# Two graph attention layers over 2708 nodes: weight rows on ScalarE's DMA queue, and layer 0 started with block 1

## The chip, the cores and the metric

The kernel runs on one core of one Trainium2 chip. Five engines with instruction streams of their own share the core's memory: TensorE (PE, matrix products), VectorE (DVE), ScalarE (ACT), GpSimd (POOL) and SyncE (SP). Transfers are issued by SP, ACT or POOL and carried by 16 DMA engines. The metric is device time in microseconds (us); smaller is better.

## The reference

Both layers work on 2708 nodes of 1024 float32 features, and on one symmetric 0/1 adjacency matrix in which about 0.6% of the entries are set, the diagonal always.

```python
# layer 0
f = x @ Wf + bf;  g = x @ Wg + bg
e = relu(f @ g.T)
attention = softmax(where(adj > 0, e, NEG), axis=1)
x = layernorm(x + attention @ (x @ W + bW))
# layer 1
h = x @ W1;  f1 = h @ a1;  f2 = h @ a2
e = leaky_relu(f1 + f2.T, 0.2)
attention = softmax(where(adj > 0, e, NEG), axis=1)
x = layernorm(x + relu(attention @ h))
```

## The kernel before

**Algebra.** Only the scores of neighbours are needed. Since f·g of a pair is a row of `x @ (Wf Wg^T)` (plus a row of constants) times a row of x, plus a number of the row alone, the kernel makes `M = Wf Wg^T` once, and per block of nodes one product F = xM. A score is then the dot product of a row of F with the gathered x of a neighbour.

**The stage before layer 0** (lines 194 to 500) does two things side by side. `lists(b)`, for each of 22 blocks of 128 rows of adj, loads 1354 KB (`sp.dma_start`, L405, into one of three buffers), marks the entries on ACT (`act.activation`, L407), multiplies by a ramp on POOL (L409), and picks the neighbours out on DVE (L412 to L418). `weights()` is a generator with one step per block: `turned` takes 128 rows of a weight (tile `rows`, three buffers), turns them on PE and copies the result to SBUF on ACT; `m_product(k, h)` makes a 128x512 piece of M out of 16 matmuls. `load_weights` issues the row loads two ahead, on SP (L276). So SP's queue holds, in program order, adj loads and weight rows mixed. `row_parts` on POOL splits a row (of the bias bW, and of a product with biases) into three bf16 rows; its float32 inputs and rests use the three buffers of tile `rest`. The two halves of bW are loaded at the start of `weights()` (L348 to L352).

**Order.** `InOrder` (L61) keeps the instructions of the five engines named `pe`, `dve`, `act`, `pool` and `sp` in program order, each engine for itself. The `nc.vector` and `nc.gpsimd` instructions of `lists` and `row_parts` are placed among them by the planner of the language.

**Layer 0** (lines 690 to 904). The sorted nodes are cut into block 0 of 20 nodes (32 rows, 3 gathered tiles) and 21 blocks of 128 rows in four groups of 32 rows. A tile is 128 gathered rows of x (`gather`, POOL), and 20 of them fit into `ring`; the order of gathers is that of `units`, and a slot is taken again once `sums` has read it. Per block: `load_x` fetches its rows (`xb`, one buffer), `q_dot` and `q_spread` make the number of the row alone (DVE, PE, DVE), `x_turn` turns xb on PE and copies it on ACT, `f_product` makes F into PSUM, `replicate(b, k)` copies the 32 rows of group k to all four quarters of a tile `Fr` (four ACT copies), `dots` forms the scores on DVE, one instruction per tile, `soft` makes the softmax weights (with an exponential on ACT), `sums` weighs the gathered tiles on PE, ACT scales them into `y`, `turn` turns y, `product` with Wt = W gives the rows of `x @ W`, and `close` adds x and normalises. Iteration k of the loop (L832) treats block b = k: its sums, the product with W of block b - 1 (`back`), x_turn and F of block b + 2 (`ahead`), and dots and softmax of block b + 1. Block 0 needs only one Fr; `f_small` spreads the inner dimension of its F over the four quarters of PE, copies these parts (`parts`) and adds them with a matmul by `rep`.

Transposes and small results go to `ps_t`, two PSUM buffers, and F and products to `ps_m`, two as well.

**Layer 1** (lines 907 to 992) is of the same make, with the products after the sums, and its rows come from a table T1 that layer 0 writes.

Of the kernel before, what the change touches and what calls it, by code (L numbers as in the profile page):

```python
# [8 lines left out]
F32 = mybir.dt.float32  # L9
# [97 lines left out]
def listed_path(ctx, tc, x, adj, Wf, bf, Wg, bg, W, bW, W1, a1, a2, out):  # L107
# [16 lines left out]
    Q = 4  # L124
# [69 lines left out]
    with tc.tile_pool(name="pre", bufs=1) as pre:  # L194
# [54 lines left out]
        with tc.tile_pool(name="adjp", bufs=3) as adjp, tc.tile_pool(name="cands", bufs=2) as cands, \  # L249
                tc.tile_pool(name="wt", bufs=1) as wt, tc.tile_pool(name="stage", bufs=3) as stage:  # L250

            def row_parts(rest, dst):

                for i in range(3):
                    t = pre.tile([1, 512], BF16, name="part", bufs=2)
                    nc.gpsimd.tensor_copy(t, rest)
                    nc.gpsimd.dma_start(dst[i:i + 1], t)
                    if i < 2:
                        nxt = pre.tile([1, 512], F32, name="rest", bufs=3)
                        nc.gpsimd.tensor_tensor(nxt, rest, t, op=ALU.subtract)  # L260
                        rest = nxt
# [10 lines left out]
            def load_weights(upto):  # L272
                while len(loaded) < min(upto, len(order)):
                    w, k = order[len(loaded)]
                    t = stage.tile([P, D], F32, name="rows")
                    sp.dma_start(t, w[k * P:(k + 1) * P, :])  # L276
                    loaded.append(t)

            at = iter(range(len(order)))
# [12 lines left out]
            def weights():  # L292
# [52 lines left out]
                four = pre.tile([32, P], F32, name="four")  # L345
                for i, v in enumerate((bg, bf, a1, a2)):
                    act.dma_start(four[8 * i:8 * i + 8], v.rearrange("(k p) -> k p" if i < 2 else "(k p) o -> k (p o)", p=P))
                for h in range(H):  # L348
                    half = slice(h * 512, (h + 1) * 512)
                    brow = pre.tile([1, 512], F32, name="rest", bufs=3)  # L350
                    act.dma_start(brow, bW[half].rearrange("(o d) -> o d", o=1))
                    row_parts(brow, b3[:, half])  # L352
                cols = pre.tile([P, 4, KC], F32, name="cols")
                bgc, bfc, ac = cols[:, 0, :], cols[:, 1, :], cols[:, 2:4, :]
                WgT = {0: half_tile()}
# [7 lines left out]
                for k in range(KC):  # L363
                    flush()
                    turned(WfT[:, :, k * P:(k + 1) * P])
                    if k >= 4:
                        turned(WgT[1][:, :, (k - 4) * P:(k - 3) * P])
                    m_product(k, 0)
                    yield
                flush()  # L370
                c_product(0)
# [155 lines left out]
    def product(n, xT, w, row=None):  # L527
# [9 lines left out]
                          start=(row is None and k == 0), stop=(k == KC - 1))  # L537
        return pm

    flat = lambda pm: pm.rearrange("p h d -> p (h d)")  # L540

    def scatter(table, idx, src):
# [28 lines left out]
    class Unit:  # L571
        pass

    def cut(most, turns):


        units, at = [], 0
        for b in range(NB):
            u = Unit()
            u.b, u.gs, u.at = b, groups[b], at  # L580
            u.G, u.T, u.n = len(u.gs), max(TILES[g] for g in u.gs), nrows[b]
            u.tiles = [(k, g, t) for k, g in enumerate(u.gs) for t in range(TILES[g])]
            u.col = {(k, t): m for m, (k, g, t) in enumerate(u.tiles)}
            u.tiles.sort(key=lambda m: (m[0] // turns, m[2]))
            u.sc = scores[b % 2][:, :u.G, :u.T]
            assert len(u.tiles) <= min(most, MOST)
            at += len(u.tiles)
            units.append(u)
        return units
# [101 lines left out]
    with ExitStack() as s0s:  # L691
# [2 lines left out]
        tp, frp = new_pool("tp", 2), new_pool("frp", Q)  # L694
        stp, xp, yp, jp = (new_pool(n, 1) for n in ("stp0", "xp", "yp", "jp0"))
        zs = new_pool("zp", 1).tile([P, TW], F32, name="z")
        units = cut(R0, 2)
        lay = Layer(units, [ring], D, x, stp)
        xb, q, qd, F, Fr, xTs, yTs, Wp, y, Z = ({} for _ in range(10))

# [30 lines left out]
        def f_small():  # L731


            xT = xTs.pop(0)
            pm = ps_m.tile([P, H, 512], F32, name="pm")
            for h in range(H):
                c = slice(h * 512, (h + 1) * 512)
                pe.matmul(pm[:32, h, :], ones3[0:3, :32], c3[:, c], start=True, stop=False)
                for k in range(KC // Q):
                    for p in range(Q):  # L740
                        i = p * KC // Q + k
                        pe.matmul(pm[32 * p:32 * p + 32, h, :], xT[:, i, :32], M[:, i, c],
                                  start=(k == 0 and p > 0), stop=(k + 1 == KC // Q))
            parts = frp.tile([P, D], F32, name="Fr")
            act.copy(parts, flat(pm))
            yield
            pm = ps_m.tile([P, H, 512], F32, name="pm")
            for h in range(H):
                pe.matmul(pm[:, h, :], rep, parts[:, h * 512:(h + 1) * 512], start=True, stop=True)
            Fr[0, 0] = frp.tile([P, D], F32, name="Fr")  # L750
            act.copy(Fr[0, 0], flat(pm))

        def replicate(b, k):
# [36 lines left out]
                pool.memset(z[:, D + 1:], 0.0)  # L790
            scatter(T1[:, :], ids[:m, b:b + 1], z[:m])

        load_x(0)
        load_x(1)
        load_lists(0)
        load_lists(1)

        def first_gathers(g0, g1):

            dve.tensor_scalar(SL0[:, g0:g1], SL[:, g0:g1, :], float(N - 1), None, op0=ALU.min)  # L800
            lay.gathers()

        q_dot(0)
        q_dot(1)
        lay.most = len(units[0].tiles)
        first_gathers(0, 1)
        lay.most += len(units[1].tiles)
        first_gathers(1, 5)
        x_turn(0)
        spread0, spread1 = q_spread(0), q_spread(1)  # L810
        next(spread0)
        small_f = f_small()
        next(small_f)
        x_turn(1)
        for _ in small_f:
            pass
        next(spread1)
        f_product(1)
        pool.memset(zs[:, D:], 0.0)
        load_x(2)  # L820
        load_lists(2)
        load_lists(3)
        for steps in (spread0, spread1):
            for _ in steps:
                pass
        for k in range(2):
            replicate(1, k)
        act.dma_start(Wt, W.rearrange("(k p) d -> p k d", p=P))
        dots(units[0], 0, len(units[0].tiles))
        soft(units[0])  # L830
        closing, loaded = iter(()), None
        for k, u in enumerate(units):  # L832
            nxt = units[k + 1] if k + 1 < len(units) else None
            b = u.b
            back = b - 1 if b > 0 else None
            ahead = b + 2 if b + 2 < NB else None
            po = ps_s.tile([P, H, 512], F32, name="po")
            y[b] = yp.tile([P, D], F32, name="y")
            if back is not None:
                for _ in yTs[back][1]:  # L840
                    pass
            reps = list(range(len(groups[b + 1]))) if nxt is not None else []

            first = k == 0
            for r in reps[2:] if first else reps[:1]:
                replicate(b + 1, r)
            next(closing, None)
            if loaded is not None:
                q_dot(loaded)
                loaded = None  # L850
            next(closing, None)
            for r in [] if first else reps[1:3]:
                replicate(b + 1, r)
            lay.sums(u, po, {12: [lambda s=closing: [None for _ in s]]})
            closing = iter(())
            act.activation(y[b][:u.n], flat(po)[:u.n], AF.Copy, scale=u.ri[:u.n])
            if ahead is not None:
                x_turn(ahead)
            if b + 3 < NB:
                load_x(b + 3)  # L860
                loaded = b + 3
            if back is not None:
                load_residual(back)
                Wp[back] = product(nrows[back], yTs.pop(back)[0], Wt, 32)
            spreading = iter(())
            if ahead is not None and not first:
                spreading = q_spread(ahead)
                next(spreading)
            for r in [] if first else reps[3:]:
                replicate(b + 1, r)  # L870
            if ahead is not None:
                f_product(ahead)
            if ahead == NB - 1:
                sp.dma_start(M, W1.rearrange("(k p) d -> p k d", p=P))
            yT = tp.tile([P, KC, P], F32, name="xT")
            steps = turn(y[b], nrows[b], yT)
            next(steps)
            yTs[b] = yT, steps
            if b + 4 < NB:
                load_lists(b + 4)  # L880
            if nxt is not None:
                dots(nxt, 0, len(nxt.tiles))
            for _ in spreading:
                pass
            if nxt is not None:
                soft(nxt)
            if first:
                q_dot(ahead)
                for _ in q_spread(ahead):
                    pass  # L890
                lay.most = len(lay.order)
                first_gathers(5, NSL0)
            if back is not None:
                closing = close(back)
                next(closing)
# [11 lines left out]
    with ExitStack() as s1s:  # L907
# [4 lines left out]
        x1 = [rb, u1b]  # L912
        z1 = [u2b, zp.tile([P, D], F32, name="z1")]
        more = new_pool("ring1", 1).tile([P, R1 - R0, TW], F32, name="more")
        units = cut(R1, Q)
        lay = Layer(units, [ring, more], TW, T1[:, :], stp)
        prod, yTs, y = {}, {}, {}

# [454 lines left out]
```

## Time and profile before

| | |
|---|---|
| median of 5 runs | 1829.52 us (1825.91 to 1834.27) |
| the profiled execution | 1834.62 us; span in the trace 1832.8 us; mean granted PE clock 0.953 |
| busy: PE, DVE, ACT, POOL | 1638.9, 1171.9, 623.6, 1189.2 us |
| stage before layer 0, up to the first gather | 0 to 242.3 us |
| start of layer 0, up to the turn of block 4's rows | 242.3 to 372.5 us |
| layer 0 from there to its end | to about 1200 us; PE busy 39.7 of each 40 us in most of it |
| moved by the DMA engines | 501.82 MB |

A line of the timeline has the start and the duration in us, the engine (SPq and ACTq are DMA issues), the source line (L71 for everything that `InOrder` records), the operation, out<-in with shapes, and in brackets the idle time of the engine before it and what ended it. A line of the waits has who waited for whom, the total in us, how often, and the longest. A line of the windows has start:end, the length, busy us of PE, PE's weight loads, DVE, ACT and POOL, and then the granted PE clock, the DMA share and GB/s.

### The profile page before, as it was taken

To read this page: it belongs to the slowest core of one execution; us is meant where nothing else is said; L and a number is where in the kernel's file an instruction comes from. 1 tells how busy PE (TensorE), PEld (TensorE's weight loads), DVE (VectorE), ACT (ScalarE), POOL (GpSimd) and SP (SyncE) were. 2 spreads that over 40 slices of the span, in tenths; PEclk is the share of its full clock that TensorE was granted. 3 is DMA by queue.
4 is the path that set the end of the run, shared out by engine and by line. 5 is a ranking of instruction groups with operands and counts; after the bars stand their busy time and mean duration, and the time that the engine had idled before them with its cause. 6 is when DMAs were issued, how large, how long until landed. Compare 5 with 4: busy or idle time off the path is not lost. (4 is left out here: it accounts for less than half of the span.)

```text
span 1832.8 us, 22235 instructions
## 1 busy us (share of the span) xinstructions
PE 1638.9 (89%) x6965; PEld 678.3 (37%) x6965; DVE 1171.9 (64%) x3533; ACT 623.6 (34%) x757; POOL 1189.2 (65%) x1191
## 2 busy tenths in 40 slices
PE   3999568899999999999999999738999999899995
PEld 2444223233444444444444444312333333333442
DVE  2868946878888888888898887523334424424442
ACT  3544516334454544444454555100111111111110
POOL 7558754666666666666667664047777777777741
PEclk8999878899999999999999999868999999999998
DMA  5555255667777777777767787269999999999960
GB/s 214 204 189 217 105 183 196 210 209 248 272 295 284 289 268 272 288 266 280 261 258 265 269 292 308 94 242 374 351 396 398 391 369 392 382 396 386 373 238 30
DMA packets 149979, 501.82 MB, mean 274 GB/s; under 512 B 32565, under 2 KB 32597, under 8 KB 147144
## 3 DMA queue, kind: packets, MB, share of 16 engines
q0 software_dynamic: 132032, 427.36, 63.1%
q1 hardware_dynamic: 13658, 68.30, 9.8%
q10 hardware_dynamic: 4162, 4.65, 0.7%
q8 instruction: 57, 0.93, 0.2%
q14 instruction: 70, 0.57, 0.1%
HBM read 509.64 MB, written 33.75 MB: 296 GB/s over the span
## 5 line engine op out<-in xcount | busy, mean ns | idle before, releaser
L71 POOL DMA_INDIRECT ring<-in_x_dram,SL x405 | 439.8, 1086 | 247.9 <-issue 96.0
L71 DVE SCALAR_TENSOR_TENSOR j<-ring,Fr 128x1024 bf16<-128x1024 f32 x405 | 497.8, 1229 | 92.6 <-DMA ring<-in_x_dram,SL 73.8
L71 PE MATMUL po<-ring,st 128*32 128x512 f32 x2660 | 386.0, 615 | 0.2 <-issue 0.2
L71 ACT COPY Fr<-pm 32x1024 f32<-32x1024 f32 (+1 forms) x338 | 339.1, 1003 | 27.0 <-PE pm L71 22.5
L71 POOL DMA_INDIRECT ring<-T,SL x260 | 258.5, 994 | 85.9 <-issue 45.2
L71 PE MATMUL pm<-Wt,xT 128*128 128x512 f32 (+1 forms) x704 | 313.7, 598 | 0.0
L71 PE MATMUL pm<-M,yT 128*128 128x512 f32 (+1 forms) x704 | 307.9, 595 | 0.3 <-ACT yT L71 0.3
L71 PE MATMUL pm<-M,xT 128*128 128x512 f32 (+1 forms) x704 | 305.3, 610 | 0.3 <-ACT xT L71 0.3
L71 ACT ACTIVATE scores<-scores 128x24 f32<-128x24 f32 (+5 forms) x44 | 9.8, 222 | 651.7 <-DVE scores L71 651.7
L71 PEld LDWEIGHTS pm<-M,yT 128*128 128x128 f32 (+1 forms) x704 | 129.5, 186 | 178.2 <-issue 177.6
L71 PEld LDWEIGHTS po<-ring,st 128*32 128x32 f32 x2660 | 111.4, 114 | 226.2 <-issue 222.1
L71 PEld LDWEIGHTS pm<-Wt,xT 128*128 128x128 f32 (+1 forms) x704 | 127.6, 186 | 159.5 <-issue 159.3
L71 PEld LDWEIGHTS pm<-M,xT 128*128 128x128 f32 (+1 forms) x704 | 125.2, 188 | 153.4 <-issue 152.8
L71 POOL DMA_INDIRECT more<-T,SL x145 | 144.6, 997 | 44.7 <-issue 27.7
L409 POOL TENSOR_TENSOR adj<-adj,iota 128x2708 f32<-128x2708 f32 (+3 forms) x23 | 130.4, 5676 | 53.2 <-ACT adj L71 53.2
L71 DVE TENSOR_SCALAR scores<-ring,f1q 128x2 f32<-128x2 f32 (+5 forms) x98 | 21.8, 237 | 200.7 <-DMA ring<-T,SL 200.4
L412 DVE MAX8 cand<-adj 128x8 f32<-128x136 f32 (+2 forms) x440 | 97.1, 285 | 56.8 <-POOL adj L409 56.8
L71 ACT ACTIVATE y<-po,ri 128x1024 f32<-128x1024 f32 (+1 forms) x44 | 49.0, 1113 | 237.2 <-PE po L71 228.5
L71 PE MATMUL pm<-halfT,WfT 128*128 128x512 f32 x256 | 117.8, 617 | 8.9 <-ACT WfT L71 8.9
L71 POOL DMA_INDIRECT SL<-LD,idq x85 | 88.1, 1037 | 25.9 <-issue 21.0
L71 PE MATMUL po<-more,st 128*32 128x512 f32 x580 | 97.8, 627 | 0.0
L71 PE MATMUL pt<-rs,stack 128*32 128x1 f32 x340 | 10.9, 182 | 86.0 <-DVE rs L71 57.7
(190 smaller groups left out, 1397.1 us busy)
## 6 DMA issues: line engine op xcount, KB each, us to landing
adj<-in_adj_dram SPq DMA_DIRECT2D x21, 1354.0 KB
X1S<-z SPq DMA_DIRECT2D x20, 512.0 KB
ring<-in_x_dram,SL POOLq DMA_INDIRECT x405, 6.2
u1b<-X1S SPq DMA_DIRECT2D x11, 512.0 KB
rb<-X1S SPq DMA_DIRECT2D x10, 512.0 KB
ring<-T,SL POOLq DMA_INDIRECT x260, 6.8
rows<-in_L_gnn_Wg_dram SPq DMA_DIRECT2D x8, 512.0 KB
rows<-in_L_gnn_Wf_dram SPq DMA_DIRECT2D x8, 512.0 KB
```

Of the source, the lines that this page charges most:

```text
L71: made = self.tc.keep_in_program_order(op(*args, **kwargs))
L409: nc.gpsimd.tensor_tensor(k[:n, cut], k[:n, cut], iota[:n, cut], op=ALU.mult)
L412: nc.vector.max(cand[:n, s, :], k[:n, s * SEG:min((s + 1) * SEG, N)])
```

## The change

- **Weight rows.** `load_weights` issues its 24 loads on ACT; SP's queue of this stage holds the 22 adj loads alone.
- **bW.** The load and the `row_parts` of each half of bW move from the start of `weights()` into its steps k = 2 and k = 5.
- **Order of layer 0.** `cut` takes an order, here 1, 0, 2, 3, ..., and the loop takes `back`, `ahead` and `nxt` from it. Loads, lists, x_turn and F of block 1 come ahead of those of block 0. x_turn(2) and F(2) move ahead of the loop. In the first iteration (now block 1) x_turn, F, and the product with W are left out; q of block 2 and `load_x(3)` come at its end, after the lists of block 4. The gathers of block 2 are released ahead of the first softmax instead of at the end of the first iteration.
- **F of block 1** is copied as 32 copies of 32x512, columns 0 to 511 of all four groups first; in the second half, group 1 is copied by DVE and the rest by ACT.
- **`f_small`** uses a general `split_product`, run through at once by `whole`, after F(1) and its copies; its parts go to the buffer of `y` and its result to `zs`.

```diff
-                    sp.dma_start(t, w[k * P:(k + 1) * P, :])
+                    act.dma_start(t, w[k * P:(k + 1) * P, :])
...
-                for h in range(H):
-                    half = slice(h * 512, (h + 1) * 512)
-                    brow = pre.tile([1, 512], F32, name="rest", bufs=3)
-                    act.dma_start(brow, bW[half].rearrange("(o d) -> o d", o=1))
-                    row_parts(brow, b3[:, half])
...
                     m_product(k, 0)
+                    if k in (2, 5):
+                        half = slice(k // 3 * 512, k // 3 * 512 + 512)
+                        brow = pre.tile([1, 512], F32, name="rest", bufs=3)
+                        act.dma_start(brow, bW[half].rearrange("(o d) -> o d", o=1))
+                        row_parts(brow, b3[:, half])
                     yield
...
+    def split_product(xT, w, parts, row=None):
+        pm = ps_m.tile([P, H, 512], F32, name="pm")
+        for h in range(H):
+            c = slice(h * 512, (h + 1) * 512)
+            if row is not None:
+                pe.matmul(pm[:32, h, :], ones3[row:row + 3, :32], rows3[row:row + 3, c], start=True, stop=False)
+            for k in range(KC // Q):
+                for p in range(Q):
+                    i = p * KC // Q + k
+                    pe.matmul(pm[32 * p:32 * p + 32, h, :], xT[:, i, :32], w[:, i, c],
+                              start=(k == 0 and (row is None or p > 0)), stop=(k + 1 == KC // Q))
+        act.copy(parts, flat(pm))
+        yield
+        pm = ps_m.tile([P, H, 512], F32, name="pm")
+        for h in range(H):
+            pe.matmul(pm[:, h, :], rep, parts[:, h * 512:(h + 1) * 512], start=True, stop=True)
+        return pm
+
+    def whole(steps):
+        while True:
+            try:
+                next(steps)
+            except StopIteration as end:
+                return end.value
...
-        units = cut(R0, 2)
+        seq = [1, 0, *range(2, NB)]
+        units = cut(R0, 2, seq)
...
+            pm = whole(split_product(xTs.pop(0), M, yp.tile([P, D], F32, name="y"), 0))
+            Fr[0, 0] = zs[:, :D]
             act.copy(Fr[0, 0], flat(pm))
...
+        load_x(1)
+        load_x(0)
+        load_lists(1)
+        load_lists(0)
+        q_dot(1)
         q_dot(0)
-        q_dot(1)
         lay.most = len(units[0].tiles)
+        first_gathers(1, 5)
+        x_turn(1)
+        spread0, spread1 = q_spread(0), q_spread(1)
+        next(spread1)
+        load_x(2)
+        load_lists(2)
+        lay.most += len(units[1].tiles)
         first_gathers(0, 1)
...
         x_turn(0)
...
         f_product(1)
         pool.memset(zs[:, D:], 0.0)
-        load_x(2)
-        load_lists(2)
         load_lists(3)
-        for steps in (spread0, spread1):
+        next(spread0)
+        for steps in (spread1, spread0):
             for _ in steps:
                 pass
-        for k in range(2):
-            replicate(1, k)
+
+        for k in range(Q):
+            Fr[1, k] = frp.tile([P, D], F32, name="Fr")
+        for h in range(H):
+            c = slice(h * 512, (h + 1) * 512)
+            for k in range(Q):
+                take = dve.tensor_copy if h > 0 and k == 1 else act.copy
+                for p in range(Q):
+                    take(Fr[1, k][32 * p:32 * p + 32, c], F[1][32 * k:32 * k + 32, h, :])
+        f_small()
+        x_turn(2)
+        f_product(2)
         act.dma_start(Wt, W.rearrange("(k p) d -> p k d", p=P))
         dots(units[0], 0, len(units[0].tiles))
+        lay.most = len(lay.order)
+        first_gathers(5, NSL0)
         soft(units[0])
...
-            if ahead is not None:
+            if ahead is not None and not first:
                 x_turn(ahead)
...
-            if ahead is not None:
+            if ahead is not None and not first:
                 f_product(ahead)
...
                 q_dot(ahead)
                 for _ in q_spread(ahead):
                     pass
-                lay.most = len(lay.order)
-                first_gathers(5, NSL0)
+                loaded = seq[k + 3]
+                load_x(loaded)
```

## The prediction

> **What bounds the kernel now.** The windows say that the bulk of layer 0 is PE-bound (39.7 busy us of 40), so what counts is when that stretch is reached. I therefore read the timeline of the two stretches ahead of it, and the waits of SP's queue in the first.
>
> ```profile
> 420.00:460.00 40.00, 39.71 (x159) 15.75 (x159) 34.51 (x79) 16.50 (x19) 24.79 (x25) 1.00 0.66 228
> ```
>
> ```profile
> SPq L71 <- PE pt L71: 96.7, 16, 16.2
> ```
>
> ```profile
> 21.37 1.07 ACT L71 COPY halfT<-pt 128x512 f32<-128x512 f32 x2 [10.91 <-POOL rest L260]
> ...
> 26.18 0.42 SPq L71 DMA_DIRECT2D adj<-in_adj_dram  x1
> ...
> 34.14 2.46 ACT L71 ACTIVATE adj<-adj 128x2708 f32<-128x2708 int32 x1 [6.05 <-DMA adj<-in_adj_dram]
> ...
> 37.22 8.86 PE L71 MATMUL pm<-halfT,WfT 128*128 128x512 f32 x16 [8.07 <-ACT WfT L71]
> ...
> 71.87 0.33 SPq L71 DMA_DIRECT2D rows<-in_L_gnn_Wg_dram  x1
> 72.30 0.37 SPq L71 DMA_DIRECT2D adj<-in_adj_dram  x1
> ...
> 79.02 2.46 ACT L71 ACTIVATE adj<-adj 128x2708 f32<-128x2708 int32 x1 [5.12 <-DMA adj<-in_adj_dram]
> ...
> 83.69 1.15 PE L71 MATMUL pt<-ident,rows 128*128 128x128 f32 x8 [2.67 <-ACT WfT L71]
> ...
> 106.88 1.97 PE L71 MATMUL pt<-ident,rows 128*128 128x128 f32 x8 [3.43 <-ACT WfT L71]
> ...
> 206.93 2.46 ACT L71 ACTIVATE adj<-adj 128x2708 f32<-128x2708 int32 x1 [2.03 <-POOL rest L260]
> ```
>
> ACT stands 10.9 us behind the second half of bW; PE's transposes stand with it, SP's next weight row waits for them, and adj of block 1, next in SP's queue, goes out at 26.2. M starts at 37.2. At 72.3 and again later adj follows a weight row by 0.4 us; ACT and then PE wait. From 108.6 to 211.5 PE hardly stops. The lists end at 231.
>
> ```profile
> 272.11 4.04 ACT L71 COPY Fr<-pm 32x1024 f32<-32x1024 f32 x4 [13.87 <-PE pm L71]
> ...
> 281.40 7.83 PE L71 MATMUL po<-ring,st 128*32 128x512 f32 x12 [0.21 <-issue]
> ...
> 305.91 1.00 POOL L71 DMA_INDIRECT xb<-in_x_dram,ids  x1 [18.63 <-PE pt L71]
> ...
> 310.25 1.23 DVE L71 SCALAR_TENSOR_TENSOR j<-xb,rb 128x1024 bf16<-128x1024 f32 x1 [3.35 <-DMA xb<-in_x_dram,ids]
> ...
> 348.23 1.11 PE L71 MATMUL pt<-ident,y 128*128 128x128 f32 x4 [3.53 <-DVE q L71]
> ...
> 352.34 0.29 PE L71 MATMUL pt<-rs,stack 128*32 128x1 f32 x8 [3.00 <-DVE rs L71]
> ...
> 372.54 1.09 PE L71 MATMUL pt<-ident,xb 128*128 128x128 f32 x8
> ```
>
> At the start of layer 0 PE idles 8.9 us after F(1), and 6.5 at block 2. x_turn(4), at 372.5, is my mark: in both kernels F of 1 to 3, the sums of 0 to 2, and one W product lie before it.
>
> **What the Trainium skill says.** "DMA: Bandwidth & Descriptors", Anatomy of one DMA: a semaphore wait is made by the issuing sequencer, ahead of dispatch. Agreed: SP's 96.7 us. The same page, Issuing engines are not separate DMA queues: SP's and ACT's transfers share the 16 engines, so two queues gain no bandwidth. "TensorE: Matmul & The Clock Gate", What's actually happening: PE falls to half clock after some 3.4 us idle and needs as long to recover. Here it showed 0.50 from 280 to 284, 0.69 in the next 4, 1.00 then: about 2.9 us lost per pause. "PSUM — Partial Sum Buffer", PSUM bank collisions: an engine may read one bank while PE writes another; the halves of F are two banks. No copy of before shows that.
>
> **The stage before layer 0.** SP issues adj 0 to 2 at once. ACT issues rows 0 to 2 after its wait for adj 0, at about 8.4 (bW went out there at 8.33). adj 0 and one row, 1.88 MB, landed in the 7 us after 1; at that rate, shared with adj 1 and 2, I put the rows at 13, 16 and 19. Row 3 is issued behind the first copies (16), lands at 20, and is copied by 23. ACT marks block 1 (2.65), copies WfT (1.08), and M starts at 26.9 instead of 37.2: 10.3 gained. The 24 issues cost ACT 0.35 each, 8 us of an engine half idle here, and a row's slot is free when ACT gets there, since ACT has copied its predecessor. Cover gone: 8 us.
>
> The PE stalls of 2.67 and 3.43 go, with the slow M products behind them (8.73 and 8.90 for 7.03, and 1.0 in transposes): 10.4. After that PE's steps are full as before. At the end adj 20 was issued at 200.05, behind weight rows; ACT's 2.03 wait ends when it lands 6.8 later (the releaser named, POOL, is the coincidence). Its slot was free by about 191, so 2.0 more. Lists keep up: DVE needs 7.4 a block, and 12 blocks from 114 end at 203, under the 208 that follows. bW's `row_parts` (7 us of POOL each, hidden before in POOL's idle time at 18 to 32) now meet steps of 8.3 to 9.4 with 5.95 of POOL work: 2.3 to 3.4 spare a step absorb each half within three; uncovered they cost up to 14. Sum: 10.3 + 10.4 + 2.0 = **22.7 gained**.
>
> **The start of layer 0**, on before's clock. x_turn(1) runs at 246.7 (landing 4.35 after the issue at 242.3). x_turn(0)'s second transpose needs the ps_t buffer of spread1, whose reader q(1) is behind the clamp of block 0's list on DVE: list landed at 253.1, q(1) done 253.6 (the wait that cost 3.53 at 348). F(1) starts at 254.2, not 257.2, PE cold: 14.9 + 2.9, end 272.0; its first half ends at 264.6. ACT's 16 first copies at 0.587 (1.76 for three of rb) end at 274.0, group 0's second half at 276.4, all at 281; group 1's second half, four DVE copies unseen before, I bound at 0.6 to 1.2 each: hidden either way, as DVE is idle. dots(1), 15 of 1.27, end at 295.4, soft (4.2) at 299.6.
>
> `f_small`, before hidden under the lists' landing, is now exposed: PE 272.0 to 276.9, then a wait for ACT's parts (1.01) to 282.2, cold sums by rep 3.0, Fr copy, x_turn(2); F(2) 287 to 303. sums(1) 303.1 to 310.2, y (1.1), exponential, q of block 2, sums(0) 314.8 to 320. (exp(0) is behind y on ACT; q_dot(2) behind soft(0) on DVE.)
>
> Now the new stall. `load_x(3)` stands on POOL behind 15 gathers, each waiting for a slot that sums(1) frees, and four list gathers. Free from 305, at 1.3 each: 324.5, then 329.7. xb(3) lands 4.35 later, at 334. On PE x_turn(3) is ahead of the W product of block 1 and F(3): **14 us idle**. On DVE q_dot(3) is ahead of all dots(2). Then 2 + 14.9 + 2 (cold), F(3) to 368.2; DVE: 335.7 + 20 x 1.27 + 4.2 = 365.3, just in time; sums(2) 369.2 to 386.4 (17.2, which is 20.17 less the cold 2.9). x_turn(4): 386.4 against 372.5, **13.9 lost**. In accounts: 24 + 3 x 2.9 of idle and cold against 16.6 + 2 x 2.9, plus `f_small` 4.9 and rests, less 3 for the earlier F(1). Wt's load, issued 12 later on ACT, is needed at 336: hidden. Later iterations issue the same work in the same order, PE-bound, and absorb nothing; layer 1 is unchanged.
>
> **Sum.** -22.7 + 13.9 = -8.8 on the profiled 1834.6 (span 1832.8): 1825.8. The median lies 5.1 below that execution, so 1829.5 - 8.8 = **1820.7**.
>
> **Rivals.**
> 1. The stall for xb(3) is hidden (gathers quicker, or freed earlier): nothing lost at layer 0, 1807. For: POOL is idle from 295. Against: the slots are read only by sums(1). Chance 0.16.
> 2. Copies of the first half wait for all of F(1): +7.4, 1828. For: before's copies waited for both halves, which they read. Against: on adj block 0, DVE started after the first of two POOL halves. 0.09.
> 3. The weights change does less than it says: adj is early, but PE's stalls move to ACT's queue, and only the head's 10.3 and the tail's 2.0 come: +1.6, 1831. 0.08.
> 4. Slower: POOL's gathers ahead of `load_x(3)` take 2.0 instead of 1.3 (single ones of before did, 319.6 and 357.6). 19 x 0.7 = 13.3 added to the stall: +4.5; from 2.06 on it is beyond 0.3%. With it, up to 1843. 0.15.
> My forecast has 0.52, itself 1813 to 1828.
>
> **Numbers.** 0.3% (5.5 us) is about what a measurement of this kernel can tell. Forecast: 0.44 faster, 0.08 same. Rival 1 faster; rival 2 same; rival 3 half same, half slower; rival 4 0.12 slower, 0.03 same. Faster 0.60, same 0.24, slower 0.16. The range goes from rival 1 to the beginning of rival 4: 1807 to 1835.
>
> **What would show it.** adj 0 to 2 issued by 2; M's first product near 27; no PE wait over 2 us between there and the last u product; lists ending near 208; F(1) starting 12 after the first gather; a wait of PE for xb of 12 to 16 behind sums(0), and an idle DVE with it; x_turn(4) some 9 us earlier than 372.5. It is wrong if lists follow DVE or POOL rather than PE, or if x_turn(3) does not wait.

## The result, and the profile after

The change made the kernel slower: 1837.98 us median against 1830.25 us for the kernel before beside it, a ratio of 1.0046 with the interval 1.0038 to 1.0054. That is 8.4 us lost (0.0046 x 1830; the medians differ by 7.7), where 8.8 us were forecast to be won. Of the five groups of experiments below, each on another chip, four met a state in which every kernel, the one before too, took 2027 to 2052 us, with pauses in the engines' instruction streams, so times are read as ratios to the kernel before of the same group, and lengths inside a trace mainly from the one group in which that kernel took 1830 us.

First the windows of the kernel after (start:end, length, busy us of PE, PE's weight loads, DVE, ACT and POOL, granted PE clock, DMA share, GB/s), and the row of SP's waits that answers to the 96.7 us for PE.

```profile
310.00:330.00 20.00, 6.60 (x14) 3.38 (x15) 6.90 (x13) 8.17 (x10) 13.88 (x14) 0.50 0.62 196
...
420.00:460.00 40.00, 39.71 (x156) 16.69 (x158) 33.59 (x78) 16.51 (x20) 27.17 (x25) 1.00 0.65 211
```

```profile
SPq L71 <- DVE cand L412: 173.8, 19, 16.6
```

The bulk of layer 0 is as full as before: 39.71 us of 40. So it is again a matter of when it is reached. The stretch from 310 to 330 is new: PE works 6.6 us of 20, at half clock. SP waits for DVE, the last reader of an adj buffer, and no longer for PE.

The timeline of the kernel after, in the stage before layer 0 (start us, length us, engine, line, operation, in brackets the idle time before it and what ended it):

```profile
0.82 34.29 SPq L71 DMA_DIRECT2D adj<-in_adj_dram  x5
...
14.69 5.39 PE L71 MATMUL pt<-ident,rows 128*128 128x128 f32 x24 [14.69 <-DMA rows<-in_L_gnn_Wg_dram]
...
26.50 1.94 PE L71 MATMUL pt<-ident,rows 128*128 128x128 f32 x8 [4.72 <-DMA rows<-in_L_gnn_Wf_dram]
...
28.26 8.00 PE L71 MATMUL pm<-halfT,WfT 128*128 128x512 f32 x16
...
186.22 2.47 ACT L71 ACTIVATE adj<-adj 128x2708 f32<-128x2708 int32 x1
...
221.21 0.15 DVE L495 TENSOR_SCALAR ids<-pt 32x1 int32<-32x1 f32 x1 [0.81 <-PE pt L71]
...
223.16 1.11 POOL L71 DMA_INDIRECT xb<-in_x_dram,ids  x1 [21.66 <-DVE ids L499]
```

adj goes out from 0.8, M starts at 28.3 instead of 37.2, the two waits of PE of 2.67 and 3.43 are gone, block 20 is marked at 186.2 instead of 206.9, and the first gather of layer 0 starts at 223.2 instead of 242.3: 19.2 us earlier. Now its start:

```profile
232.59 9.93 PE L71 MATMUL pm<-M,xT 128*128 128x512 f32 x16
...
242.77 7.13 PE L71 MATMUL pm<-M,xT 128*128 128x512 f32 x16
...
249.94 11.73 ACT L71 COPY Fr<-pm 32x512 f32<-32x512 f32 x20 [17.41 <-PE pm L71]
...
261.71 2.78 DVE L71 COPY Fr<-pm 32x512 f32<-32x512 f32 x4 [11.23 <-ACT Fr L71]
...
264.52 4.71 ACT L71 COPY Fr<-pm 32x512 f32<-32x512 f32 x8 [2.85 <-DVE Fr L71]
...
270.32 3.78 PE L71 MATMUL pm<-y,rep 128*128 128x512 f32 x4 [15.77 <-ACT y L71]
...
318.53 1.00 POOL L71 DMA_INDIRECT xb<-in_x_dram,ids  x1 [0.30 <-issue]
...
322.87 1.23 DVE L71 SCALAR_TENSOR_TENSOR j<-xb,rb 128x1024 bf16<-128x1024 f32 x1 [21.33 <-DMA xb<-in_x_dram,ids]
...
322.98 1.08 PE L71 MATMUL pt<-ident,xb 128*128 128x128 f32 x4 [16.37 <-DMA xb<-in_x_dram,ids]
...
326.06 9.28 PE L71 MATMUL pm<-Wt,xT 128*128 128x512 f32 x16
...
375.73 1.09 PE L71 MATMUL pt<-ident,xb 128*128 128x128 f32 x8
```

Four things are to be seen. F(1)'s first half ends at 242.5, the second at 249.9, and ACT begins to copy at 249.94, not at 242.5. DVE's four copies begin when ACT's 20 are done, and ACT's last eight when DVE's are done. PE stands 15.8 us until ACT has copied the parts of `f_small`, behind all of these copies. And PE and DVE stand 16.4 and 21.3 us for the rows of block 3, issued by POOL at 318.5. The turn of block 4's rows, the prediction's mark, comes at 375.7, 152.6 us behind the first gather; before, it was 372.5 and 130.2. So the profiled executions show 19.2 won, 22.4 lost: 3.2 us. From the mark to the end of layer 0 (the last `fq` product starts at 1211.26, before at 1206.42) 1.6 more are lost, and 0.5 come back in layer 1, which makes the 4.3 by which the spans differ (1837.1 and 1832.8). That is less than the 8.4 of the ratio: the profiled execution of before is 4.4 above the median of its runs, that of after 1.2 above. Where these 4.4 may lie is taken up below.

### The profile page after: what moved, and what is told of

It is laid out like the page before. It is cut to its first block, busy times and chain, and to the rows that moved or that the text cites. A ratio compares the mean times of both kernels' runs of the same rounds, so it can differ in the third digit from the quotient of the medians.

```text
span 1837.1 us, 22242 instructions
## 1 busy us (share of the span) xinstructions
PE 1634.2 (89%) x6965; PEld 679.7 (37%) x6965; DVE 1174.0 (64%) x3537; ACT 623.4 (34%) x769; POOL 1181.7 (64%) x1191
## 5 line engine op out<-in xcount | busy, mean ns | idle before, releaser
L71 POOL DMA_INDIRECT ring<-in_x_dram,SL x405 | 430.3, 1062 | 295.1 <-PE po L71 100.7
L71 PE MATMUL po<-ring,st 128*32 128x512 f32 x2660 | 381.8, 611 | 0.0
L71 PE MATMUL pm<-halfT,WfT 128*128 128x512 f32 x256 | 113.4, 598 | 0.9 <-ACT WfT L71 0.9
L71 POOL DMA_INDIRECT SL<-LD,idq x85 | 87.4, 1028 | 25.8 <-issue 21.8
L71 DVE TENSOR_SCALAR scores<-more,f1q 128x3 f32<-128x3 f32 (+2 forms) x67 | 15.4, 239 | 107.2 <-DMA more<-T,SL 105.3
```

Of the source, the lines that this page charges most:

```text
L71: made = self.tc.keep_in_program_order(op(*args, **kwargs))
```

## The experiments

**Theory.** The stage before layer 0 gains about what was forecast. The start of layer 0 loses 10 us more than forecast (22.4, and 1.5 by which the first gather follows the first ids later than before, against 13.9), since the copies of F(1) wait for the whole PSUM tile (7.4 us, the length of the second half) and DVE's four copies are done in turn with ACT's (2.85). **Rivals:** the stage gains much less than 20; or the start of layer 0 loses only the forecast 13.9; or the late copies and the late rows of block 3 hide each other, and mending one brings nothing.

In the table, length is the time from the first gather to the turn of block 4's rows in the profiled execution. The runs of the group at 1830 us are in bold. xb_two_c has four executions only and no ratio; after_again, two_tiles_b, xb_two_b and pre_only_c gave no time.

| run | median us | before beside it | ratio (95%) | first gather | length |
|---|---|---|---|---|---|
| pre_only | 2024.26 | 2051.98 | 0.9851 (0.9774 to 0.9928) | 219.6 | 148.0 |
| layer0_only | 2064.49 | 2051.98 | 1.0129 (1.0058 to 1.0199) | 238.9 | 155.4 |
| xb_early | 2016.83 | 2051.98 | 0.9819 (0.9782 to 0.9856) | 218.5 | 141.2 |
| two_tiles | 2041.68 | 2051.98 | 0.9960 (0.9906 to 1.0014) | 225.5 | 156.3 |
| pre_only_b | 1998.49 | 2027.26 | 0.9818 (0.9750 to 0.9886) | 218.4 | 145.8 |
| xb_early_b | 2005.53 | 2027.26 | 0.9847 (0.9808 to 0.9887) | 222.1 | 141.8 |
| xb_two | 2002.19 | 2027.26 | 0.9877 (0.9845 to 0.9908) | 220.3 | 139.3 |
| pre_bw | 2018.61 | 2027.26 | 0.9940 (0.9901 to 0.9980) | 224.6 | 147.8 |
| after_third | 2043.44 | 2047.74 | 0.9959 (0.9912 to 1.0005) | 223.4 | 156.1 |
| two_tiles_c | 2057.72 | 2047.74 | 1.0145 (0.9943 to 1.0347) | 224.6 | 153.7 |
| xb_two_c | 2048.50 | 2047.74 | none | 222.0 | 139.6 |
| pre_only_d | 2025.62 | 2047.74 | 0.9923 (0.9885 to 0.9960) | 224.4 | 147.1 |
| **pre_only_e** | 1813.07 | 1830.00 | 0.9900 (0.9881 to 0.9919) | 223.3 | 128.7 |
| **layer0_only_b** | 1854.28 | 1830.00 | 1.0132 (1.0114 to 1.0150) | 237.4 | 152.2 |
| **two_tiles_d** | 1831.68 | 1830.00 | 1.0011 (0.9997 to 1.0025) | 220.0 | 143.1 |
| **xb_two_d** | 1817.26 | 1830.00 | 0.9929 (0.9911 to 0.9947) | 221.3 | 131.5 |
| late_q | 2008.78 | 2039.56 | 0.9879 (0.9837 to 0.9922) | 222.9 | 139.8 |
| pre_only_f | 2016.71 | 2039.56 | 0.9957 (0.9918 to 0.9996) | 217.8 | 149.9 |

### The two halves of the change alone

pre_only is the kernel before with the weight rows on ACT's queue and bW in steps 2 and 5; layer0_only is the kernel after with these two put back.

```diff
-                    sp.dma_start(t, w[k * P:(k + 1) * P, :])
+                    act.dma_start(t, w[k * P:(k + 1) * P, :])
...
-                for h in range(H):
-                    half = slice(h * 512, (h + 1) * 512)
...
-                    row_parts(brow, b3[:, half])
...
+                    if k in (2, 5):
+                        half = slice(k // 3 * 512, k // 3 * 512 + 512)
...
+                        row_parts(brow, b3[:, half])
```

> The kernel before with only the two edits of the stage before layer 0 (weight rows on ACT, bW moved into steps 2 and 5); layer 0 as before. Theory (the stage gains what it did in the changed kernel, 20.7 us, and layer 0 keeps its old length of 130.2 us from the first gather to the turn of block 4's rows): first gather at 221.7, that turn at 352, time 1830 - 20.7 = 1809.5. Rival (the earlier end of the lists is eaten by something later whatever layer 0 does): above 1822.

> The changed kernel with the stage before layer 0 put back as it was. Theory (the new start of layer 0 costs 23.9 us by itself: 375.7 - 372.5 + 20.7): first gather at 242.3, turn of block 4's rows at 396, time 1830 + 24 + what the tail adds (up to 4) = 1854 to 1858. Rival (start of layer 0 costs only the 13.9 that was forecast, and the rest comes from both together): 1844.

> The same kernel as the first of this kind (the two edits of the stage before layer 0 alone), on another occasion, since in the first all kernels, the one before too, had pauses in their instruction streams. Theory: first gather at 221.7, turn of block 4's rows at 352, 20.7 less than before, ratio 0.989. Rival (something later eats it): ratio above 0.995.

> Before, with the weight rows on ACT's queue and bW in steps 2 and 5 and nothing else. Theory (that half of the change gains 20.7 us, and all of it reaches the end): first gather near 221, 130 us from there to the turn of block 4's rows as in before, ratio 0.988 to 0.990. Rival (a later start was needed for something, so layer 0 gives part of it back): 137 or more to the turn, ratio 0.993 or above.

> Before, with the weight rows on ACT's queue and bW in steps 2 and 5 and nothing else. Theory: first gather 20 to 21 us before that of the kernel before (242.3), 130 us from there to the turn of block 4's rows where the streams do not pause, ratio 0.988 to 0.990. Rival (layer 0 gives part of the gain back): 137 or more to the turn although nothing pauses, ratio 0.993 or above.

> After, with the weight rows on SP's queue and bW at the start again: the new start of layer 0 alone. Theory: first gather near 243, 152 to 154 us to the turn of block 4's rows, ratio 1.012 to 1.014 (23.9 us on 1830). Rival (the prediction's 13.9): 144 us, ratio near 1.0076.

In the group at 1830 us, pre_only_e won 18.3 us (0.0100 x 1830; 14.8 to 21.8) and layer0_only_b lost 24.2 (20.9 to 27.5). Together +5.9, and the whole change measured +8.4; the intervals allow that the halves simply add. The forecast had -22.7 and +13.9. The rival of a loss of 13.9 is out. In this group pre_only_e has the old start of layer 0 in 128.7 us, so it keeps the stage's gain, and layer0_only_b has the new one in 152.2, as in the kernel after. The timeline of layer0_only_b:

```profile
82.84 1.15 PE L71 MATMUL pt<-ident,rows 128*128 128x128 f32 x8 [2.36 <-ACT WfT L71]
83.83 7.03 PE L71 MATMUL pm<-halfT,WfT 128*128 128x512 f32 x16
...
103.04 1.15 PE L71 MATMUL pt<-ident,rows 128*128 128x128 f32 x8 [2.01 <-ACT WfT L71]
104.02 7.03 PE L71 MATMUL pm<-halfT,WfT 128*128 128x512 f32 x16
...
235.46 0.15 DVE L495 TENSOR_SCALAR ids<-pt 32x1 int32<-32x1 f32 x1 [0.81 <-PE pt L71]
...
264.11 11.73 ACT L71 COPY Fr<-pm 32x512 f32<-32x512 f32 x20 [17.10 <-PE pm L71]
...
336.85 1.09 PE L71 MATMUL pt<-ident,xb 128*128 128x128 f32 x4 [16.18 <-DMA xb<-in_x_dram,ids]
```

The late copies and the wait for block 3 are there without the weights' new queue. The upper lines price the old stage anew: its two waits of PE are 2.36 and 2.01 us here, and the M products behind them take 7.03 us, full speed, where the profiled execution of before had 2.67 and 3.43 and then 8.73 and 8.90. With the same stage in its code, layer0_only_b has the first ids at 235.6, before at 242.05. So the same stage differs by 6.4 us between these two executions, 5.6 of it between 83 and 117 us, where the two stalls are; that is more than the 4.4 by which the profiled execution of before lies above its median. The two kernels differ behind that stage, so that executions of before itself spread as much is likely and not shown.

The other groups agree on the sign of each half. On the size of the second they don't speak with one voice: layer0_only, the only other run of it alone, has nearly the same ratio, 1.0129, in a wide interval, but by the traces the old start of layer 0 is longer there as well (145.8 to 149.9 in the pre_only runs, where 128.7 to 130.2 were expected), and the new one is 155.4 in layer0_only. In the timeline of pre_only_d, ACT stands 19.60 us ahead of the copies of F(1), ended by nothing that the trace shows on this core; in that of pre_only_e it stands 13.87 there, until PE is done:

```profile
272.83 4.04 ACT L71 COPY Fr<-pm 32x1024 f32<-32x1024 f32 x4 [19.60 <-remote]
```

```profile
253.43 4.04 ACT L71 COPY Fr<-pm 32x1024 f32<-32x1024 f32 x4 [13.87 <-PE pm L71]
```

This may be why the kernel after, run once more in such a group, was no slower than before:

> The kernel after as it is, as the measure for the other three of this call. Theory (the stage before layer 0 gains 20.7, the start of layer 0 loses 23.9): ratio to before 1.002 to 1.006, first gather near 223, the turn of block 4's rows near 376, that is 152 to 153 us after the first gather; PE waits some 16 us for xb of block 3. Rival (the start of layer 0 loses only 13.9, and what was measured is the chip's doing): 144 us and a ratio near 0.995.

Measured 0.9959, with 156.1 us from first gather to the mark, PE's wait for xb 12.5. Its own start of layer 0 is 3.5 us longer than in the first profile, that of the old kernel (pre_only_d) 147.1 instead of 128.7. The expectation of 1.002 to 1.006 failed. What makes the streams pause in these groups isn't known. Of what follows, only pre_bw and late_q rest on them.

### bW alone

pre_bw is the kernel before with bW in steps 2 and 5 and nothing else; the weight rows stay in SP's queue.

```diff
-                for h in range(H):
-                    half = slice(h * 512, (h + 1) * 512)
...
+                    if k in (2, 5):
+                        half = slice(k // 3 * 512, k // 3 * 512 + 512)
```

> The kernel before with bW alone moved into steps 2 and 5; weight rows stay on SP. Theory (the head's 10 us come from ACT's stop behind bW, the waits at 83.7 and 106.9 from SP's mixed queue): adj of block 1 is issued near 13, M starts near 24, and PE's waits for ACT between 70 and 110 stay (5 to 10 us in all): 12 to 14 less than before, ratio 0.993. Rival (the mixed queue also holds the head): M starts after 32, under 6 less.

PE's timeline in pre_bw, and after it SP's wait for PE (us in total, times, longest):

```profile
25.57 8.55 PE L71 MATMUL pm<-halfT,WfT 128*128 128x512 f32 x16 [7.58 <-ACT WfT L71]
...
71.13 1.15 PE L71 MATMUL pt<-ident,rows 128*128 128x128 f32 x8 [2.07 <-ACT WfT L71]
...
91.38 1.15 PE L71 MATMUL pt<-ident,rows 128*128 128x128 f32 x8 [2.08 <-ACT WfT L71]
```

```profile
SPq L71 <- PE pt L71: 82.4, 16, 15.5
```

M starts at 25.6, where the old stage started it at 37.0 (layer0_only, in a group with pauses too) and the pre_only runs at 24.9 to 29.4. So the start of bW was what held the head. The waits of PE stay, as short as in layer0_only_b (2.07 and 2.08, below the 5 to 10 us expected), and SP still waits 82.4 us for PE. What the queue adds isn't settled. The first gather is at 224.6, that of pre_only_b beside it at 218.4, which would leave 6 us to the queue; but the pre_only runs alone lie between 217.8 and 224.4. The ratios, 0.9940 and 0.9818, put more on the queue, with wide intervals. The weight rows on ACT's queue were not run alone.

### Two PSUM tiles for F(1)

The halves of F(1) go into two tiles, so that a copy can wait for its half alone. Order and number of the copies stay.

```diff
-        f_product(1)
+        F1 = [ps_m.tile([P, H, 512], F32, name="pm"), ps_s.tile([P, H, 512], F32, name="po")]
...
+                pe.matmul(F1[h][:, h, :], xT1[:, k, :], M[:, k, c], start=False, stop=(k == KC - 1))
...
-                    take(Fr[1, k][32 * p:32 * p + 32, c], F[1][32 * k:32 * k + 32, h, :])
+                    take(Fr[1, k][32 * p:32 * p + 32, c], F1[h][32 * k:32 * k + 32, h, :])
```

> The changed kernel with the two halves of F(1) in two PSUM tiles instead of two halves of one. Theory (a reader of one half waits for the last write to the whole tile): ACT's first copy starts at the end of the first half, 242.5 instead of 249.9, everything behind it is 7.4 earlier, time 1830.5; ACT and DVE still take turns inside the second tile. Rival (the copy waits for PE for another reason, such as the instruction that signals): the first copy stays at 249.9, time 1838.

> After, with the halves of F of block 1 in two PSUM tiles. Theory (copies wait for the whole PSUM tile): ACT's first copy directly behind the first half, some 7.4 us earlier against the first gather than in the kernel after; everything behind it moves along, so 144 to 146 us from first gather to the turn of block 4's rows, and a ratio 0.004 below that of the kernel after in this call. Rival (the copies start early, but the sums of block 1 are held by something else): first copies early, and the length still 151 or more.

> After, with the halves of F of block 1 in two PSUM tiles. Theory: 144 to 146 us from first gather to the turn of block 4's rows where the streams do not pause, ratio 0.999 to 1.002 (1.0046 less 7.4 us). Rival (the sums of block 1 are held by something else): 151 or more, ratio 1.003 to 1.006.

The timeline of two_tiles_d:

```profile
237.83 9.39 ACT L71 COPY Fr<-pm 32x512 f32<-32x512 f32 x16 [8.71 <-PE pm L71]
...
238.04 7.13 PE L71 MATMUL po<-M,xT 128*128 128x512 f32 x16
...
249.60 2.78 DVE L71 COPY Fr<-po 32x512 f32<-32x512 f32 x4 [3.85 <-ACT Fr L71]
...
252.41 4.71 ACT L71 COPY Fr<-po 32x512 f32<-32x512 f32 x8 [2.84 <-DVE Fr L71]
...
258.21 3.78 PE L71 MATMUL pm<-y,rep 128*128 128x512 f32 x4 [8.39 <-ACT y L71]
...
310.58 1.08 PE L71 MATMUL pt<-ident,xb 128*128 128x128 f32 x4 [16.42 <-DMA xb<-in_x_dram,ids]
```

ACT copies the first half while PE writes the second, and PE's wait behind the copies falls from 15.77 to 8.39: 7.4 us, as the theory has it. So what the copies had waited for was the write of the other half. The time falls from 1.0046 to 1.0011 of before, by 6.4 us, and the length from 152.6 to 143.1; of the 2.1 beyond 7.4, 1.3 is a first half of F(1) that took 8.62 us here and 9.93 in the other. The wait for block 3 is the same 16.4: the two costs add and don't hide each other. Inside the second tile ACT and DVE still take turns, at 2.84 us.

In the first two runs of this edit the copies started early too (243.59 and 242.23, behind 8.63 and 8.62 us of waiting for PE), but ACT paused later and the length stayed at 156.3 and 153.7; the expected length failed there, and was met in the group at 1830 us.

### The rows of block 3 earlier

xb_early is the kernel after with q of block 2 ahead of the copies of F(1), and the load of block 3's rows right behind the turn of block 2's.

```diff
+        q_dot(2)
...
         x_turn(2)
+        load_x(3)
...
-                q_dot(ahead)
...
-                load_x(loaded)
```

xb_two is the same edit with the two tiles.

> The changed kernel with q of block 2 (its dot product on DVE) moved ahead of the copies of F(1), and the load of block 3's rows right behind the turn of block 2's rows, so that it stands on POOL ahead of the gathers that wait for the sums of block 1. Theory (PE's 16.4 us wait for xb and the cold clock behind it are one cause): the wait is gone, sums of block 2 start when PE is free, near 338.5 instead of 358.4, the turn of block 4's rows at 356, time 1838 - 20 = 1818. Rival (the gathers of block 2 and DVE's dots behind them are the bound, and the wait only moves there): the turn at 368 or later, gain under 8.

> The same kernel as the first of this kind (q of block 2 and the load of block 3's rows early), again. Theory (the wait for xb with the cold clock behind it is 20 of the loss): PE has no wait for xb over 2 us, turn of block 4's rows at 356, ratio to before 0.993. Rival (the gathers of block 2 bound it): turn at 368 or later, ratio 1.000 or above.

> The changed kernel with both: block 3's rows early, and the halves of F(1) in two PSUM tiles. Theory (the two losses are in series on PE): 20 + 7.4 = 27.4 less than the changed kernel, turn of block 4's rows at 348.5, ratio to before 0.989. Rival (with one gone, DVE's dots of block 2 are the bound, and the other is worth nothing): as with the early rows alone, 0.993.

> After, with both repairs: two PSUM tiles for F of block 1, and the rows of block 3 loaded directly behind the turn of block 2. Theory (7.4 for the copies and 16 for the rows are the two costs): 130 to 135 us from first gather to the turn of block 4's rows unless DVE's dots of block 2 become the bound, PE with no wait for xb over 1 us, ratio to before 0.985 to 0.990. Rival (the two costs hide each other): 140 or more, ratio 0.992 to 0.996.

> After, with both repairs. Theory: 130 to 135 us from first gather to the turn of block 4's rows, no wait of PE for xb over 1 us, ratio 0.988 to 0.992. Rival (the two costs hide each other, or DVE's dots of block 2 become the bound): 140 or more, ratio 0.993 or above.

The timeline of xb_two_d:

```profile
257.83 1.23 DVE L71 SCALAR_TENSOR_TENSOR j<-xb,rb 128x1024 bf16<-128x1024 f32 x1 [9.48 <-DMA xb<-in_x_dram,ids]
...
262.15 4.72 ACT L71 COPY Fr<-po 32x512 f32<-32x512 f32 x8 [9.97 <-DVE Fr L71]
...
267.97 3.78 PE L71 MATMUL pm<-y,rep 128*128 128x512 f32 x4 [15.54 <-ACT y L71]
...
303.95 1.09 PE L71 MATMUL pt<-ident,xb 128*128 128x128 f32 x8
```

The turn of block 3's rows follows sums(0) without a wait. But the edit brought a wait of its own: q of block 2, which I had put ahead of DVE's copies, waits for the rows of block 2, DVE's copies wait with it, and ACT stands 9.97 us where two_tiles_d has 2.84. So 7.1 us of what the tiles had won are lost again (15.54 against 8.39). The length is still 131.5, 11.6 less than two_tiles_d, and the time 1.0011 to 0.9929, 15 us less, with intervals that allow the 11.6. Had the 7.1 not been lost, the rows would by this sum have been worth 18.7 in length: the wait of 16.4 and some 2 us by which the product behind it ran cold (9.28 for 7.13 in the kernel after, 9.04 in two_tiles_d). The expected 130 to 135 us was met, the ratio of 0.988 to 0.992 just missed. xb_early and xb_early_b show no wait of PE for xb either, at 141 to 142 us with ACT pausing.

### Both repairs, with that q behind the dots of block 1

late_q is two_tiles with q of block 2 and the load of block 3's rows right behind the dots of block 1.

```diff
         dots(units[0], 0, len(units[0].tiles))
+        q_dot(2)
+        load_x(3)
...
-                q_dot(ahead)
...
-                load_x(loaded)
```

> After, with two PSUM tiles for F of block 1, and q of block 2 and the load of block 3's rows directly behind the dots of block 1. Theory (7.4 us for the copies and some 20 for the rows with the cold clock behind them, each separable): 123 to 126 us from first gather to the turn of block 4's rows, less than the 128.7 of pre_only; ratio 0.986 to 0.990. Rival (DVE's dots of block 2 become the bound): 130 or more, ratio 0.991 or above.

> The stage before layer 0 alone, as the measure for the other run. Theory: as before, 128.7 us from first gather to the turn of block 4's rows, ratio 0.988 to 0.992.

ACT's timeline in late_q:

```profile
255.42 4.72 ACT L71 COPY Fr<-po 32x512 f32<-32x512 f32 x8 [2.85 <-DVE Fr L71]
...
271.75 1.01 ACT L71 COPY y<-pm 128x1024 f32<-128x1024 f32 x1 [11.61 <-remote]
```

ACT's wait for DVE is back at 2.85, and PE has no wait for xb. But this pair met an occasion with pauses: ACT stood 11.61 us right behind the copies, so the expected length of 123 to 126 (131.5 less 7.1) was not seen: 139.8. Beside pre_only_f at 149.9, in the same group, it is 10 us shorter, and the ratios stand 0.9879 to 0.9957, with intervals that barely overlap. The version with the misplaced q is not ahead of the old order: xb_two has 0.9877 beside 0.9818 of pre_only_b, xb_two_d 0.9929 beside 0.9900 of pre_only_e. Whether the new order of layer 0, with both repairs, beats the old one at 1830 us therefore stays open. What is shown there: pre_only_e (0.9900) and xb_two_d (0.9929) beat both the kernel before and the kernel after.

## Why the prediction was wrong

Each half went the way that was forecast, their balance did not: -22.7 and +13.9 were forecast, -18.3 and +24.2 measured, so the sum changed its sign. The stall for block 3 was foreseen; what the copies of F(1) wait for was not.

- **The step that failed: "its first half ends at 264.6. ACT's 16 first copies at 0.587 ... end at 274.0".** They were to start at the end of the first half; they start at the end of the second, 7.4 us later. This was rival 2, at 0.09, with the right mechanism and price; its evidence, that before's copies waited for both halves, was put aside because they read both, and the counter-evidence came from another tile, adj, with other engines. That one engine may read one half while PE writes the other is right, and two_tiles_d shows ACT and PE so (ACT reads pm from 237.83 on, PE writes po from 238.04). But what decides is not what the memory permits; it is what a copy waits for in this program. For adj it was the half, for this PSUM tile it is the whole.
- **"four DVE copies unseen before, I bound at 0.6 to 1.2 each: hidden either way, as DVE is idle".** They took 0.7 each, inside the bounds, but not hidden: ACT's last eight wait 2.85 us for them. ACT alone would have needed four more copies of 0.58, 2.3; no run tried that, so the net cost of the turns is put at 0.5 by this sum alone. I asked whether DVE had time, and not who stands behind DVE. 13.9 + 7.4 + 2.85 = 24.2 is what layer0_only_b measured; in an interval of 20.9 to 27.5, the agreement to the tenth is luck. Smaller errors nearly cancel in it: F(1) started 8.9 us behind the first gather, not 11.9; the wait for block 3 was 16.4, not 14; and the first gather itself, now that of block 1's rows, started 1.5 us later behind the first ids than before (1.80 against 0.29).
- **The stage: 22.7, measured 18.3 by the median.** The head came at 28.3, not 26.9: the first rows landed by 14.7, not 13, and PE waited 4.7 us for the first row of Wf. The term of 10.4 for the stalls of PE was probably too large, in a way that the profile of before could not show alone: in layer0_only_b the same stalls cost 4.4 and leave the clock as it is, and so they do in layer0_only (2.62 and 2.08) and pre_bw. The prediction took the gain off the median as if the profiled execution's 5.1 us above it lay elsewhere; layer0_only_b points to the very stage whose stalls were priced. The first ids of the old stage came at 235.6 and 242.05 in two traces, a mean of 238.8; of the new one at 221.4, 223.0, 218.2 and 219.5 in the traces of after, pre_only_e, two_tiles_d and xb_two_d, a mean of 220.5. The difference of the means is the measured 18.3, but with two and four traces that lie up to 6.4 and 4.8 us apart it could as well have been some us off.
- **Right:** adj issued at 0.8; no wait of PE over 2 us from M's first product to the end of the weights; lists behind PE; `row_parts` of bW absorbed; POOL's gathers at 1.3 us apart, so not rival 4; x_turn(3) behind the rows of block 3 and DVE idle with it; dots of block 2 just in time (sums(2) waited 0.16 us); layer 1 unchanged. Rival 1 (the stall hidden) and rival 3 (the PE stalls moved) are out.
- **The sum again,** with the measured terms: 1829.5 - 18.3 + 24.2 = 1835.4; measured 1837.98, with some 2.6 us left, 0.7 of it from the median of before (1830.25 beside the result); the rest the two halves' intervals cover and no run separates.

## What to carry to other kernels

In this program, copying a product by halves brought nothing while both halves lay in one PSUM tile. Where that is so, give each half a tile of its own, and see in the trace whether the first copy's wait ends with the first half. Work handed to an idle engine inside a chain is hidden only if nothing on the first engine waits for it. And before a stall is priced from one profiled execution that lies above its median, ask whether the stall is where the surplus lies; here 6 of 10.4 us were not there in another execution of the same stage.

## What the runs showed of the hardware

- ACT and DVE, copying different 32-partition parts of one PSUM tile, took turns: DVE began when ACT's first run was done (11.23 us), ACT went on when DVE was done (2.85), and the same in layer0_only_b, two_tiles_d and late_q. The Trainium skill ("PSUM — Partial Sum Buffer", PSUM bank collisions raise a hardware error) allows two engines in one bank at once in different quadrants of 32 partitions, which these parts are; no run here shows it. The waits are semaphore waits of the program, by all signs its guard of the tile, though no run gave ACT and DVE tiles of their own; whether the memory would have borne both at once was not tried.
- PE's clock: in before, PE paused 2.67 us up to 83.69, at a granted clock of 1.00; the clock fell to 0.50 near 85.1, when PE had worked again for 1.4 us, and was back at 88.5, so that the product behind the pause took 8.73 us instead of 7.03. A pause of 2.62 in the same place (layer0_only) and one of 2.85 at 851 us (layer0_only_b) left the clock at 1.00, while one of 2.09 at 987 us (pre_bw) was followed by 0.50. So the length of a pause of this size does not decide; what does stays open. The Trainium skill ("TensorE: Matmul & The Clock Gate", What's actually happening) puts the fall behind an idle window of some 3.4 us; by the trace's idle times it came sooner here. Behind long waits one product of 7.13 took 8.62 (two_tiles_d) to 9.93 us (after), so 1.5 to 2.8 us are lost in it, at most nearly the 2.9 that the prediction used.
- The same stage in the code took 235.6 and 242.05 us up to its first ids, in two kernels whose executions all lie within 0.5% of their medians: two waits of PE, 2.36 and 2.01 or 2.67 and 3.43, and what the clock did behind them, make 5.6 of the 6.4 us.
